# Row means taken off the down weights once, and the last tiles of the last segment summed chunk by chunk

## The chip, the cores and the metric

The kernel runs on one core of one Trainium2 chip. The metric is the device time of one execution in microseconds (us), the median of several runs. The engines are called as in the profile: PE (TensorE), DVE (VectorE), ACT (ScalarE), POOL (GpSimd), SP (SyncE, which issues most DMAs).

## What is computed

The input `u` is 4 sequences of 1024 tokens with 256 features. Two blocks follow, each between two layernorms without gain or bias, with a residual sum:

```python
x = x + layernorm(mamba2(layernorm(x)))
x = x + layernorm(ffn(layernorm(x)))

gate = x @ Wg.T;  up = x @ Wu.T            # Wg, Wu: 2048 x 256, dequantized from 4-bit codes
out  = (gelu_tanh(gate) * up) @ Wd.T       # Wd: 256 x 2048, dequantized from 4-bit codes
layernorm(x) = (x - mean(x)) / sqrt(var(x) + 1e-5)
```

The change concerns the very last layernorm, the one over the 256 outputs of `ffn`.

## The kernel before, in words

**Recorded, then ordered.** The kernel does not call the engines directly. A `Recorder` notes every operation (`add`, line 158), finds out which earlier operations it depends on, gives it a modelled duration (`weigh`, line 227) and, in `issue` (line 260), a list scheduler sets the order of each engine's instructions. So all instructions stand at line 347 in the profile, and are told apart by the names of their tiles. Among the operations that are ready, the one with the lowest `rank` (line 363) goes first: operations of the feed-forward part that are not on PE have rank 5, its PE products 25 + 10 s for segment s, the down products 27 + 10 s, the mixer of segment 2 has 10, the unpacking of the down weights 24. When two operations on different engines touch the same PSUM bank, the recorder orders them, also if both only read (line 185). Buffers come from pools (line 84) and are handed out nearly in the order in which they were asked for; pool "yo" has one buffer, "act" three, "fo" two.

**Segments.** The 4096 tokens are cut into 9 segments (line 25): two of 256 tokens, then seven of 512. For each there is a mixer (the Mamba-2 block, line 646) and a feed-forward part (`ffn`, line 960). A chunk is 128 tokens, so a segment has NC = 2 or 4 chunks.

**Feed-forward part.** The 2048 hidden features are NN = 16 tiles of 128. In segments 0 and 1, `widen(n)` makes one tile: gate and up products on PE, gelu on ACT, the product of both on DVE, and `narrow((n,))` adds the tile's share of the down product. From segment 2 on, `widen_pair(j)` makes tiles j and j + 8 at once by a scheme with seven products, and `narrow((j, j + 8))` follows. `narrow` loops over the chunks and adds, for each, the given tiles to `pd`, a half of a PSUM bank: chunks 0 and 1 share one bank, chunks 2 and 3 the other. A matmul in float32 appears as two PE instructions in the profile. The weights of the down product are `wd`, 128 partitions x 2 x 2048; tile n = 2 tt + par is the slice `wd[:, par, 256 tt : 256 tt + 256]`, a hidden feature per partition and the 256 outputs along it.

**Finish.** `finish(i)` (line 1059) does the last layernorm of a chunk: `bn_stats` and `bn_aggr` on DVE give mean and variance of `pd`, two POOL operations on one column give `q = (var + eps)^-0.5`, DVE computes `(pd - mean) * q` into "fo", POOL adds the residual, SP stores. The way out of the mixer (`way_out`, line 904) does the corresponding layernorm of the first block with a mean square only: its weights `wo` have their row means taken off in `prepare_wo` (line 572). Its steps are Square with an accumulated sum on ACT, two small POOL operations and one DVE operation.

**Unpacking.** `unpack` (line 585) turns the 4-bit codes into float weights. For the down weights it is recorded after the first four steps of segment 0's `ffn` (line 1123). Its codes lie in `big`, its signs in the "yo" buffer, and it writes `wd` in pieces of 512 columns: the first two on DVE, the others on POOL.

Of the kernel before, what the change touches and what calls it, by code (L numbers as in the profile page):

```python
# [12 lines left out]
AF = mybir.ActivationFunctionType  # L13
ALU = mybir.AluOpType
PSUM = bass.MemoryType.PSUM

P = 128
EPS = 1e-5
NB, L, DM = 4, 1024, 256
# [5 lines left out]
SEGS = [(0, 0, 256), (0, 256, 256)] + [(b, 0, 512) for b in range(1, NB)] + \  # L25
# [11 lines left out]
NN = MLP // P  # L37
# [336 lines left out]
def mamba_ffn_kernel(  # L374
# [19 lines left out]
    r = Recorder(tc.nc)  # L394
# [4 lines left out]
    def pool(name, shape, k=1, ahead=2, of=None, dtype=F32):  # L399
        of = of or sb  # L400
        return Pool([of.tile(shape, dtype, name=f"{name}{j}") for j in range(k)], ahead)

    def fixed(name, shape):
        return pool(name, shape).get()
# [30 lines left out]
    def get(tag):  # L435
        return pools[tag].get()
# [37 lines left out]
    for name, shape, src in (("dtb", [P, NH], dt_bias), ("aneg", [P, NH], a_log),  # L474
                             ("cw", [P, NF, 4], conv_w), ("cb", [P, NF], conv_b),
                             ("dsk", [P, DI // P], d_skip), ("nw", [P, DI // P], norm_w)):
        t = small_loads[name] = fixed(name, shape)
# [49 lines left out]
    wd = fixed("wd", [P, 2, MLP])  # L527
# [19 lines left out]
    def stats_of(rows, who="m"):  # L547

        n = len(rows)
        mv = get("mv" + who)[:, :n, :]  # L550
        for i, row in enumerate(rows):
            st = get("st" + who)
            r.vector.bn_stats(st, row)
            r.vector.bn_aggr(mv[:, i, :], st)
        return mv
# [29 lines left out]
    def unpack(pack, scale, room, dst, spare, own, by_product=True):  # L585

        w, sc = room[:, :MLP].bitcast(I32), room[:, MLP:]
        r.sync.dma_start(out=w, in_=pack)
        if by_product:
            few = dst.rearrange("p k n -> p (k n)")[:8, :MLP]
            r.sync.dma_start(out=few, in_=scale)
        else:
            r.sync.dma_start(out=sc, in_=scale.unsqueeze(1).to_broadcast([8, 16, MLP]))
        by, lo, hi = [spare[:, k * 512 : (k + 1) * 512] for k in range(3)]
        sg = get("yo").rearrange("p c t -> p (c t)").bitcast(I32)  # L600
        r.scalar.copy(by.bitcast(U8), w.bitcast(U8).rearrange("p (n k) -> p n k", k=4)[:, :, 0])
        by, lo, hi = by.bitcast(I32), lo.bitcast(I32), hi.bitcast(I32)
        r.vector.tensor_scalar(lo, by, 0x07070707, 2, ALU.bitwise_and, ALU.logical_shift_left)
        r.vector.tensor_scalar(sg, by, 4, 0x80808080 - (1 << 32),
                               ALU.logical_shift_left, ALU.bitwise_and)
        r.vector.tensor_tensor(lo, lo, sg, ALU.bitwise_or)
        r.vector.tensor_scalar(hi, by, 2, 0x1C1C1C1C, ALU.logical_shift_right, ALU.bitwise_and)
        r.vector.tensor_scalar(sg, by, 0x80808080 - (1 << 32), None, ALU.bitwise_and)
        r.vector.tensor_tensor(hi, hi, sg, ALU.bitwise_or)
        for q in range(4):  # L610
            cols = slice(q * 512, (q + 1) * 512)
            by_column = sc[:, cols]
            if by_product:
                bank = banks_d.get()
                r.tensor.matmul(bank, lhsT=spread, rhs=few[:, cols], start=True, stop=True)
                if q < own:
                    by_column = bank
                else:
                    r.scalar.copy(by_column, bank)
            for par, codes in enumerate((lo, hi)):  # L620
                (r.vector if q < own else r.gpsimd).tensor_tensor(
                    dst[:, par, cols], codes.bitcast(F8)[:, cols], by_column, ALU.mult)

    def weight_sums():
# [333 lines left out]
    def ffn(s):  # L960
# [3 lines left out]
        if s < 2:  # L964
            at = big[s].rearrange("p (n t) -> p n t", t=T)
            inter = [[at[:, n, i * P : (i + 1) * P] for i in range(NC)] for n in range(NN)]
        else:


            at = [big[0][:, k * 2 * TMAX : (k + 1) * 2 * TMAX] for k in range(4)]  # L970
# [4 lines left out]
        def widen(n):  # L975
            cols = slice(n * P, (n + 1) * P)
            bank = banks_f.get("full")


            parts = NC if s == 0 else 1  # L980
            step = T // parts
            for i in range(parts):
                for m, w in enumerate((wg, wu)):
                    for kk in range(2):
                        r.tensor.matmul(bank[:, m * T + i * step : m * T + (i + 1) * step],
                                        lhsT=w[:, kk, cols],
                                        rhs=xfT[s][:, kk, i * step : (i + 1) * step],
                                        start=(i == 0 and m == 0 and kk == 0),
                                        stop=(kk == 1), skip_group_check=True)
            a = get("act")  # L990
            r.scalar.activation(a, bank[:, :T], AF.Gelu_apprx_tanh)
            r.vector.tensor_tensor(at[:, n, :], a, bank[:, T : 2 * T], ALU.mult)

        def fetch(k):
            r.sync.dma_start(out=blocks[k % 2], in_=stock[k])
# [40 lines left out]
        def widen_pair(j):  # L1036
            a = big[1][:, j % 4 * 2 * TMAX : (j % 4 + 1) * 2 * TMAX]
            for k, bank in enumerate(seven(0, j)):
                r.scalar.activation(a[:, k * TMAX : (k + 1) * TMAX], bank, AF.Gelu_apprx_tanh)
            for k, bank in enumerate(seven(1, j)):  # L1040
                cols = slice(k * TMAX, (k + 1) * TMAX)
                r.vector.tensor_tensor(at[j % 4][:, cols], a[:, cols], bank, ALU.mult)

        def narrow(tiles):


            r.key = ("down", s)
            if not tiles[0]:
                v_["pd"] = [banks_d.get() for i in range(0, NC, 2)]
            for i in range(NC):  # L1050
                pd = v_["pd"][i // 2][:, i % 2 * DM : (i % 2 + 1) * DM]
                for n in tiles:
                    tt, par = divmod(n, 2)
                    r.tensor.matmul(pd, lhsT=inter[n][i], rhs=wd[:, par, tt * DM : (tt + 1) * DM],
                                    start=(n == 0 and i % 2 == 0), stop=(n == NN - 1),
                                    skip_group_check=True)
            r.key = ("ffn", s)

        def finish(i):
            x = xs[s]  # L1060
            pd = v_["pd"][i // 2][:, i % 2 * DM : (i % 2 + 1) * DM]
            om = stats_of([pd], "f")

            q = get("rsf")[:, 0:1]
            r.gpsimd.tensor_scalar(q, om[:, 0, 1:2], 1.0, EPS * 2.0 ** -12, ALU.mult, ALU.add)
            r.gpsimd.tensor_tensor(q, q, mhalf[:, 0:1], ALU.pow)
            o = get("fo")
            r.vector.tensor_scalar(o, pd, om[:, 0, 0:1], q, ALU.subtract, ALU.mult)
            r.gpsimd.tensor_tensor(o, o, x[:, i, :], ALU.add)
            r.sync.dma_start(out=out[r0 + i * P : r0 + (i + 1) * P, :], in_=o)  # L1070

        if s < 2:
            steps = [lambda n=n: widen(n) for n in range(NN)]
            steps += [lambda n=n: narrow((n,)) for n in range(NN)]
        else:
            steps = [token_sums]
            for j in range(NN // 2):
                if j % 2 == 0:
                    steps.append(lambda k=j // 2: fetch(k))
                steps.append(lambda j=j: widen_pair(j))  # L1080
                steps.append(lambda j=j: narrow((j, j + 8)))
        return steps + [lambda i=i: finish(i) for i in range(NC)]

    r.key = ("small", 0)
# [4 lines left out]
    def do(kind, s, steps):  # L1089
        for step in steps:  # L1090
            r.key = (kind, s)
            step()
# [25 lines left out]
    for s in range(ns):  # L1118
        steps = ffn(s)
        if s == 0:  # L1120
            do("ffn", 0, steps[:4])
            r.key, r.floor = ("w", 1), 24000.0
            unpack(d_pack, d_scale, big[1], wd, big[0][:, 5 * MLP // 4 :], 2, False)
            r.floor = 0.0
            steps = steps[4:]
        do("ffn", s, steps)
        if s == 0:
            r.key, r.floor = ("w", 2), 75000.0
            weight_sums()
            r.floor = 0.0  # L1130
        if s + 2 < ns:
            do("mix", s + 2, mix[s + 2])
# [52 lines left out]
```

## Time and profile before

| | us |
|---|---|
| median of 3 runs | 1045.73 |
| lowest and highest run | 1041.16 and 1045.83 |
| the profiled execution | 1042.28 |
| its span, first to last instruction | 1040.6 |
| granted TensorE clock, mean | 0.99 |
| matmuls of the down product (`d<-wd,big`) | 1024 instructions, 254.9 busy |
| first down product starts | 119.8 |
| ACT table loads | 50, 64.2 busy |

The profile comes from one execution. Its page has a table of busy time, a strip in 40 slices, the DMA queues, the chain of work that ended last, and the groups of instructions. In a group or a timeline line, `out<-in` are the names of the tiles written and read, without their numbers; `x4` says how many instructions were merged, and what stands in brackets is how long the engine had been idle before, and the instruction whose end released it. In a table of stretches each engine has its busy time and number of instructions, and then come the granted TensorE clock (1.00 is full speed), the DMA engines' busy share and GB/s. Tiles that matter: `d` are the PSUM banks of the down product, `a` and `f` the other PSUM banks, `stf`, `mvf`, `rsf` and `fo` belong to `finish`, `one` and `xn` to the mixer's way out, `act` and `big` hold hidden features.

### The profile page before, as it was taken

How to read it: one execution, taken by the hardware profiler on the slowest of the kernel's cores; microseconds unless marked ns; L12 is line 12 of the kernel's file. 1: busy time of each engine (PE TensorE's matmuls, PEld its weight loads, DVE VectorE, ACT ScalarE, POOL GpSimd, SP SyncE). 2: the span in 40 equal slices, each digit the busy share in tenths (PEclk: the TensorE clock that was granted, in tenths of full speed). 3: DMA queues.
4: the chain of work that ended last, by engine and by line, in shares of the span. 5: the costliest groups of instructions: out<-in, count | busy, mean ns of one | idle time of the engine just before them, and what ended most of it. 6: DMA issues, size and time to landing. Idle time of an engine off the chain costs nothing. (4 is left out here: it accounts for less than half of the span.)

```text
span 1040.6 us, 14518 instructions
## 1 busy us (share of the span) xinstructions
PE 1010.6 (97%) x5174; PEld 809.5 (78%) x5174; DVE 652.1 (63%) x1443; ACT 471.3 (45%) x1106; POOL 327.7 (31%) x519
## 2 busy tenths in 40 slices
PE   7989999989999999999999999999999999999996
PEld 6678877866788768876788778877787778888885
DVE  5776695457766775767665857586667765433432
ACT  4536245426663375444654726365435743331330
POOL 1754853440143222503440146102640145002002
PEclk8999999989999999999999999999999999999999
DMA  7014151414032143113312423123221430232400
GB/s 258 3 41 143 74 180 42 172 31 130 23 111 100 44 150 117 37 63 132 111 52 77 145 101 124 72 92 111 83 91 72 132 132 16 76 142 81 151 2 20
DMA packets 39456, 97.16 MB, mean 93 GB/s; under 512 B 3800, under 2 KB 29896, under 8 KB 35272
## 3 DMA queue, kind: packets, MB, share of 16 engines
q1 hardware_dynamic: 38808, 96.22, 27.1%
q8 instruction: 40, 0.66, 0.3%
q14 instruction: 32, 0.26, 0.1%
q10 hardware_dynamic: 576, 0.02, 0.0%
HBM read 84.58 MB, written 11.66 MB: 92 GB/s over the span
## 5 line engine op out<-in xcount | busy, mean ns | idle before, releaser
L347 PE MATMUL f<-wide 128*128 128x256 f32 x880 | 255.4, 384 | 0.6 <-DVE f L347 0.3
L347 PE MATMUL d<-wd,big 128*128 128x256 f32 x1024 | 254.9, 381 | 0.0
L347 PE MATMUL f<-xfT,wide 128*128 128x256 f32 (+1 forms) x1024 | 249.9, 356 | 2.6 <-ACT tail L347 1.3
L347 PEld LDWEIGHTS d<-wd,big 128*128 128x128 f32 x1024 | 189.8, 190 | 31.9 <-issue 9.2
L347 PEld LDWEIGHTS f<-xfT,wide 128*128 128x128 f32 x1024 | 172.0, 191 | 31.2 <-issue 9.2
L347 PEld LDWEIGHTS f<-wide 128*128 128x128 f32 x880 | 161.5, 191 | 35.2 <-issue 12.7
L347 DVE TENSOR_TENSOR f<-f,sums 128x256 f32<-128x256 f32 x216 | 92.5, 429 | 97.9 <-PE f L347 89.9
L347 PE MATMUL a<-xnT,win 128*128 128x512 f32 (+1 forms) x300 | 136.5, 584 | 1.3 <-DVE xw L347 1.0
L347 DVE SCALAR_TENSOR_TENSOR xc<-a,cw,xc 128x511 f32<-128x511 f32 (+1 forms) x135 | 97.9, 727 | 8.9 <-ACT tail L347 6.6
L347 ACT ACTIVATE big<-f 128x512 f32<-128x512 f32 x108 | 63.0, 597 | 79.8 <-DVE f L347 56.0
L347 PEld LDWEIGHTS a<-xnT,win 128*128 128x128 f32 x300 | 55.0, 190 | 44.7 <-issue 37.1
L347 DVE TENSOR_TENSOR big<-big,f 128x512 f32<-128x512 f32 x108 | 72.8, 683 | 26.9 <-PE f L347 16.5
L347 ACT ACTIVATE e<-e,ncs 128x128 f32<-128x128 f32 x240 | 73.9, 390 | 20.8 <-POOL e L347 20.7
L347 ACT COPY f<-f 128x256 f32<-128x256 f32 x104 | 37.5, 361 | 79.8 <-PE f L347 68.7
L347 POOL TENSOR_TENSOR state<-state,dec 128x512 f32<-128x512 f32 x24 | 25.0, 1043 | 149.6 <-PE a L347 128.7
L347 ACT ACT_TABLE_LOAD x50 | 64.2, 1283 | 3.6 <-issue 2.8
L347 POOL TENSOR_SCALAR_AFFINE_SELECT e<-e 128x1024 f32<-128x1024 f32 x30 | 33.1, 1104 | 102.1 <-DMA e<-rows 101.8
L347 POOL TENSOR_SCALAR rsf<-mvf 128x1 f32<-128x1 f32 x32 | 6.9, 215 | 179.3 <-DVE mvf L347 154.2
L347 ACT ACTIVATE xc<-a,cb,cw 128x512 f32<-128x512 f32 (+1 forms) x45 | 34.3, 761 | 50.8 <-PE a L347 50.8
L347 PE MATMUL a<-wo,y 128*128 128x256 f32 x232 | 55.8, 382 | 1.3 <-DVE x L347 1.2
L347 ACT ACTIVATE th<-xc 128x512 f32<-128x512 f32 (+1 forms) x54 | 31.6, 586 | 45.1 <-DVE xc L347 31.1
L347 POOL TENSOR_TENSOR y<-xc,dsk 128x512 f32<-128x512 f32 x32 | 33.6, 1064 | 56.1 <-DVE xc L347 28.1
(242 smaller groups left out, 1402.0 us busy)
## 6 DMA issues: line engine op xcount, KB each, us to landing
wide<-stock SPq DMA_DIRECT2D x28, 1792.0 KB, 7.4
e<-rows SPq DMA_DIRECT2D x30, 512.0 KB, 4.0
r<-rows SPq DMA_DIRECT2D x54, 128.0 KB, 4.0
stock<-sums SPq DMA_DIRECT2D x8, 512.0 KB, 2.8
out_dram<-fo SPq DMA_DIRECT2D x32, 128.0 KB, 1.7
x<-in_u_dram SPq DMA_DIRECT2D x7, 512.0 KB, 3.9
stock<-wide SPq DMA_DIRECT2D x6, 512.0 KB, 6.5
win<-in_w_in_dram SPq DMA_DIRECT2D x2, 512.0 KB, 6.4
```

The source lines that it names most:

```text
L347: getattr(getattr(self.nc, st.queue), st.name)(*[real(a) for a in st.args], **{k: real(a) for k, a in st.kwargs.items()})
```

## The change

There are three edits.

1. A new function `centre_wd`, called once, right after the down weights are unpacked. For each of the 16 tiles of `wd` ACT sums the 256 outputs of every hidden feature, scaled by -1/256, into one column (the element-wise result goes to a "yo" buffer and is not used), and then adds that column to the tile in place. The down product of such weights has a mean of zero over its 256 outputs.
2. `finish` takes the mean square of `pd` on ACT (Square with an accumulated sum; the element-wise result goes to an "act" buffer and is not used), computes `q` on POOL as before, and makes `pd * q + x` in one DVE operation. The mean, `bn_stats`, `bn_aggr` and the POOL addition are gone.
3. In the last segment, the tiles of the pairs 6 and 7 are no longer added by two calls of `narrow`, each over all chunks, but by one call over four tiles: all four for chunk 0, then for chunk 1, and so on.

```diff
+    def centre_wd():
+        n = NN
+        mean = fixed("centre", [P, n])
+        at = lambda tt, par: wd[:, par, tt * DM : (tt + 1) * DM]
+        for k in range(n):
+            junk = get("yo").rearrange("p c t -> p (c t)")[:, :DM]
+            r.scalar.activation(junk, at(*divmod(k, 2)), AF.Identity, scale=-1.0 / DM,
+                                 accum_out=mean[:, k : k + 1])
+            r.scalar.activation(at(*divmod(k, 2)), at(*divmod(k, 2)), AF.Identity,
+                                 bias=mean[:, k : k + 1])
...
         def finish(i):
             x = xs[s]
             pd = v_["pd"][i // 2][:, i % 2 * DM : (i % 2 + 1) * DM]
-            om = stats_of([pd], "f")
-            q = get("rsf")[:, 0:1]
-            r.gpsimd.tensor_scalar(q, om[:, 0, 1:2], 1.0, EPS * 2.0 ** -12, ALU.mult, ALU.add)
+            small = get("rsf")
+            so, q = small[:, 0:1], small[:, 1:2]
+            junk = get("act")
+            r.scalar.activation(junk, pd, AF.Square, scale=1.0 / math.sqrt(DM), accum_out=so)
+            r.gpsimd.tensor_scalar(q, so, 1.0, EPS * 2.0 ** -12, ALU.mult, ALU.add)
             r.gpsimd.tensor_tensor(q, q, mhalf[:, 0:1], ALU.pow)
             o = get("fo")
-            r.vector.tensor_scalar(o, pd, om[:, 0, 0:1], q, ALU.subtract, ALU.mult)
-            r.gpsimd.tensor_tensor(o, o, x[:, i, :], ALU.add)
+            r.vector.scalar_tensor_tensor(o, pd, q, x[:, i, :], ALU.mult, ALU.add)
             r.sync.dma_start(out=out[r0 + i * P : r0 + (i + 1) * P, :], in_=o)
...
-                steps.append(lambda j=j: narrow((j, j + 8)))
+                if s < len(SEGS) - 1 or j < NN // 2 - 2:
+                    steps.append(lambda j=j: narrow((j, j + 8)))
+                elif j == NN // 2 - 1:
+                    steps.append(lambda j=j: narrow((j - 1, j + 7, j, j + 8)))
...
             unpack(d_pack, d_scale, big[1], wd, big[0][:, 5 * MLP // 4 :], 2, False)
+            centre_wd()
```

## The prediction

> **What bounds the kernel now.** First the page's table of busy time, then the busy time by stretches, then the instructions in order of time around the two places that the change touches.
>
> ```profile
> PE 1010.6 (97%) x5174; PEld 809.5 (78%) x5174; DVE 652.1 (63%) x1443; ACT 471.3 (45%) x1106; POOL 327.7 (31%) x519
> ```
>
> PE (TensorE) is the bound. It is idle for 30.0 us in all: 8.6 after its last matmul, and the other 21.4 in a few places (9.7 in the first 90 us, 1.5 at 113, 4.8 between 215 and 230, the rest in crumbs below 0.5). Work taken off DVE or POOL, or put on ACT, moves the time only in those places, or where it makes a new one. The stretches that matter (columns: span, busy us and instructions of PE, weight load, DVE, ACT, POOL; granted clock; DMA):
>
> ```profile
> 112.00:120.00 8.00, 6.47 (x57) 6.43 (x57) 7.32 (x12) 1.75 (x6) 7.75 (x11) 1.00 0.01 2
> 120.00:125.00 5.00, 5.00 (x29) 4.36 (x28) 2.30 (x7) 1.77 (x5) 3.04 (x6) 1.00 0.26 107
> 125.00:130.00 5.00, 5.00 (x26) 3.48 (x25) 0.40 (x3) 0.83 (x2) 2.17 (x4) 1.00 0.45 165
> 130.00:140.00 10.00, 10.00 (x42) 7.69 (x41) 9.65 (x18) 4.43 (x8) 5.82 (x8) 1.00 0.50 180
> 215.00:230.00 15.00, 10.16 (x43) 7.65 (x42) 8.53 (x25) 3.59 (x12) 6.56 (x16) 0.82 0.20 54
> 1032.00:1040.60 8.60, 0.00 (x0) 0.00 (x0) 2.88 (x8) 0.00 (x0) 5.07 (x10) 0.78 0.18 61
> ```
>
> Here the reader sees room on ACT from 112 to 140 (8.8 us busy of 28), where the centring must go; an idle, slowed PE around 220; and a tail in which PE does nothing and POOL is busiest. The tail in order of time (start, duration):
>
> ```profile
> 1014.98 17.00 PE L347 MATMUL d<-wd,big 128*128 128x256 f32 x78
> 1030.29 0.76 DVE L347 BATCH_NORM_STATS2 stf<-d 128x6 f32<-128x256 f32 x2 [11.17 <-PE d L347]
> ...
> 1032.02 0.76 DVE L347 BATCH_NORM_STATS2 stf<-d 128x6 f32<-128x256 f32 x2 [0.75 <-PE d L347]
> ...
> 1034.79 0.46 POOL L347 TENSOR_SCALAR rsf<-mvf 128x1 f32<-128x1 f32 x2
> 1035.33 1.06 POOL L347 TENSOR_TENSOR rsf<-rsf,mhalf 128x1 f32<-128x1 f32 x2
> 1035.91 1.20 DVE L347 TENSOR_SCALAR fo<-d,mvf,rsf 128x256 f32<-128x256 f32 x2 [2.10 <-POOL rsf L347]
> 1036.53 1.40 POOL L347 TENSOR_TENSOR fo<-fo,x 128x256 f32<-128x256 f32 x2
> ```
>
> PE ends at 1031.98 with 78 instructions of the last down product (a matmul is two, so 39 of them at 17.00 / 39 = 0.436 us). The finishes go by pairs: chunks 0 and 1 lie in one bank and start when both are summed, at 1030.29; chunks 2 and 3 at 1032.02. POOL decides the end: the adds of chunks 0 and 1 hold it until 1034.7, so the second pair's first POOL step waits until 1034.79, and the last add ends at 1037.93. The last store and what follows it take 1040.60 - 1037.93 = 2.67 us.
>
> **Part 1: the tail.** A finish loses on DVE bn_stats (420 ns), bn_aggr (169) and the 534 ns TENSOR_SCALAR, and on POOL the 774 ns add; it gains on ACT a Square with its accumulator and on DVE one SCALAR_TENSOR_TENSOR. The same four operations at the same size stand in the mixer's way out, here with nothing in their way:
>
> ```profile
> 221.31 0.38 ACT L347 ACTIVATE xn<-a 128x256 f32<-128x256 f32 x1 [3.85 <-DVE one L347]
> 221.59 0.20 ACT L347 ACTIVATION_READ_ACCUMULATOR xn<-a 128x1 f32 x1
> ...
> 221.86 0.19 POOL L347 TENSOR_TENSOR one<-one,one 128x1 f32<-128x1 f32 x1
> 222.13 0.55 POOL L347 TENSOR_TENSOR one<-one,mhalf 128x1 f32<-128x1 f32 x1
> ...
> 222.71 0.48 DVE L347 SCALAR_TENSOR_TENSOR x<-a,one,x 128x256 f32<-128x256 f32 x1 [0.48 <-POOL one L347]
> ```
>
> So one chain is 223.19 - 221.31 = 1.88 us. The question is whether two chunks of one bank overlap. In the way out DVE reads the bank for q, and ACT's Square reads other columns of it only afterwards, though it needs nothing of q:
>
> ```profile
>   ACT xn L347: 50.3, 24
> ```
>
> That is the list of who waited for tile "one": ACT's Squares stood 50.3 us in 24 waits that ended with DVE's read. I take it that chunk 3's Square waits in the same way for chunk 2's DVE output. The second pair: 1032.02 + 1.88 = 1033.90, 0.05 to hand over, + 1.88 = 1035.83, + 2.67 = 1038.50. That is **-2.1 us** against 1040.60. The first pair is done 16 instructions earlier when the last 16 matmuls go chunk by chunk (8 of a bank, 3.5 us, where it was 1.73 us), so its chains run from about 1028.5 to 1032.4. By the old order they would run from 1030.29, mixed with the second pair's on three engines that are each under 1 us busy per chunk; the reorder by itself I price at 0 to 0.3 us. PE loses nothing by it: the last inputs are written by 1019.13, 13 us before the end. The stores take two "fo" buffers; the third output comes about 3 us after the first, whose store landed in 1.7 us, so no wait is added there.
>
> The Trainium skill, page "PSUM — Partial Sum Buffer", section "PSUM bank collisions raise a hardware error", says that two engines may not touch one bank and quadrant at once, reads against reads included, and that guards go by bank. That speaks against the change, which puts two reading engines where one had both reads: with the rule the sum is the -2.1 us above, without it the -3.2 of rival 1. The 50.3 us agree with it.
>
> **Part 2: centring, once.** 16 tiles of 128x256, two ACT operations each. The nearest rows: the Square with accumulator is 0.47 us to the end of the read (221.31 to 221.79); the scaled activation of "wo" at this size is 514 ns with a pointer operand. About 1.0 us a tile with the hand-over, 16 us in all. The tiles share one "yo" buffer, handed out in order, so sums go tile 0 to 15. Tile 0 is unpacked by 113.1, tiles 0 to 3 by about 114, tile 4 by 115.6; the last DVE write into wd, which I take to be tiles 5 and 7, ends at 120.0. On ACT, with the gelus between, tiles 0 to 4 are done by about 119, 5 to 7 by 123.5, then the mixer's copies (123.56 to 124.9) and tiles 8 to 15 by about 134.5. What PE wants, and when:
>
> ```profile
> 119.78 1.03 PE L347 MATMUL d<-wd,big 128*128 128x256 f32 x4
> ...
> 130.64 4.48 PE L347 MATMUL d<-wd,big 128*128 128x256 f32 x20
> ```
>
> Segment 0 has two chunks, so a tile is four PE instructions. Tile 0 is wanted at 119.78, 22 instructions have gone by 125.4 (into tile 5), tile 10 is wanted near 134.5, tile 11 at 136.67. Every tile is there one to five us early, so nothing is lost; but a gelu or copy may stand up to 0.5 us behind a centring operation, and ACT may wait in order for the write that ends at 120.0. I take **+0.3**; the ends are 0 and the whole cover of 119.8 to 125.4, 22 x 0.217 = 4.8 us. Nothing else in the box of 112 to 140 moves: wd is not read before, and the next user of "yo" comes after 170. Square and Identity ran between gelus with no table load in front (xn at 103.83, xc at 129.12), so none is counted.
>
> **Part 3: the other 28 finishes.** DVE loses 0.65 us and POOL 0.77 us of each, ACT gains 0.58. They lie beside a PE that is 99% busy, and a bank held 2 us longer is wanted again only a widened pair later. Only segment 1's finish falls into an idle stretch, 216.9 to 221.7: its two POOL adds and DVE steps stand ahead of the mixer's rsm, xf and one. Taking 1.46 us from POOL and 1.3 from DVE there I put at **-0.5**; the ends are +0.5 (a Square ahead of the mixer's) and the gap itself, 4.8.
>
> **Sum** -2.1 + 0.3 - 0.5 = -2.3 us: the profiled execution's 1042.28 would become 1040.0. It lies 3.45 under the median of the runs, which spread from 1041.16 to 1045.83; a new median has the same spread, so I put the sum on the median: 1045.73 - 2.3 = **1043.4**. Less than 0.5% (5.2 us) is about what a measurement of this kernel can't tell from no change.
>
> **Rivals.** The issue order is planned from modelled costs, so all of it may shift; these are the ways that have a price.
>
> 1. Bank reads don't serialize. Chunk 3's Square follows chunk 2's by 0.5 us, only POOL's 0.82 us per chunk lies between, and its chain ends near 1034.7: -3.2 in the tail, 1042.3 in all; were chunks freed singly, not by bank, -4.0 and 1041.5. Against it: the 50.3 us, and pairs that started together at 1030.29 and 1032.02. Chance 0.12.
> 2. The stretch at 220 closes. PE is idle 4.8 us there and its clock is 0.82, which costs 10.16 x 0.18 = 1.8 us more. If a new order fills it, -6.6, with the tail and the front -8.4: 1037.3. For it: three engines wait for each other by turns there. Against: the chain is way out, statistics, xf, transposes, which all stay. Chance 0.16.
> 3. ACT is late at 120, and the time is slower. If tile 0 is centred only at 125, PE loses its filler of 4.8 us. The tiles behind it follow at 1.8 us (1.0 us each in the 56% that ACT has free from 130 to 140), so tile 10, wanted at 134.5, comes at 143, and half of the 42 instructions from 130.6 to 144.5 has no cover, 4.6 us. The gap at 220 shows what follows an idle PE: a clock of 0.82 there, 2.4 us with the ten us behind it. 11.8 - 2.6 = +9.2: 1054.9. It decides from the point where tile 0 comes 3 us after 119.78; before that the tail pays for it. For it: ACT's order is fixed beforehand, and one DVE write into wd took 1.51 us where another took 0.81. Against: ACT is busy 1.75 of the 8 us before, and segment 1's products could fill from 125 on. Chance 0.14.
>
> The forecast, a change between -4 and +1, has 0.58. Noise of the median can carry a part of it over the bound, so faster 0.21 (rival 2 and a twentieth), same 0.65, slower 0.14. The range takes in rival 2 and the forecast's spread, and stops short of rival 3's end: 1037.3 to 1049.0.
>
> **What would show it.** Tail: a gap of about 6.5 us after the last matmul; ACT's second Square of a pair released by DVE "fo" and not by PE; POOL under 0.8 us per chunk. Front: ACT busy some 16 us more between 112 and 136, no PE wait on ACT "wd". Middle: DVE 21 and POOL 25 us less, ACT 35 more, PE's sum of busy time unchanged. It is wrong if PE's idle time before the tail leaves 21.4 by more than 3 us.

## The result, and the profile after

The median is 1039.76 us (20 runs, 1035.7 to 1042.6) against 1041.76 of the kernel before on the same chip (20 runs, 1039.88 to 1045.85). The medians lie 2.0 us apart; the ratio on record, which is not that of the two medians, is 0.9977 with a 95% interval of [0.9967, 0.9988]: 2.4 us less, with an interval from 1.2 to 3.4. The profiled execution took 1041.29 us with a span of 1039.2. Its table of busy time:

```profile
PE 1012.9 (97%) x5174; PEld 811.5 (78%) x5174; DVE 634.2 (61%) x1379; ACT 506.0 (49%) x1224; POOL 302.5 (29%) x487
```

PE has the same 5174 instructions; DVE is busy 17.9 us less, POOL 25.2 less, ACT 34.7 more. Of ACT's, 7.7 us are six more table loads (56 instead of 50, 1.28 each); they come with the new finish, as e6 below has 56 without any centring, and e2, the centring alone, has 50. The tail after, in order of time:

```profile
1015.68 17.00 PE L347 MATMUL d<-wd,big 128*128 128x256 f32 x78
...
1029.33 0.38 ACT L347 ACTIVATE act<-d 128x256 f32<-128x256 f32 x1 [18.02 <-PE d L347]
...
1031.26 0.38 ACT L347 ACTIVATE act<-d 128x256 f32<-128x256 f32 x1 [1.46 <-DVE fo L347]
...
1032.78 0.38 ACT L347 ACTIVATE act<-d 128x256 f32<-128x256 f32 x1 [1.04 <-PE d L347]
...
1034.71 0.38 ACT L347 ACTIVATE act<-d 128x256 f32<-128x256 f32 x1 [1.46 <-DVE fo L347]
...
1035.28 0.19 POOL L347 TENSOR_SCALAR rsf<-rsf 128x1 f32<-128x1 f32 x1 [1.11 <-ACT act L347]
1035.55 0.55 POOL L347 TENSOR_TENSOR rsf<-rsf,mhalf 128x1 f32<-128x1 f32 x1
1036.13 0.48 DVE L347 SCALAR_TENSOR_TENSOR fo<-d,rsf,x 128x256 f32<-128x256 f32 x1 [1.45 <-POOL rsf L347]
```

The four Squares (`act<-d`) show who let each one go: the first of a bank is released by PE, the second by DVE's output of the first. One engine works at a time, down to the last DVE output at 1036.13 + 0.48 = 1036.61; the gap after the last matmul is 1039.2 - 1032.68 = 6.5 us, where it was 8.6. The stretches that answer to those of before:

```profile
112.00:120.00 8.00, 6.47 (x50) 6.08 (x50) 7.79 (x14) 3.06 (x11) 7.75 (x8) 1.00 0.16 67
120.00:125.00 5.00, 5.00 (x42) 4.82 (x41) 3.71 (x8) 4.89 (x17) 5.00 (x8) 1.00 0.01 3
125.00:130.00 5.00, 5.00 (x31) 4.00 (x30) 1.46 (x5) 4.90 (x17) 3.08 (x7) 1.00 0.26 105
130.00:140.00 10.00, 10.00 (x41) 7.01 (x41) 5.99 (x10) 8.47 (x25) 4.17 (x6) 1.00 0.73 262
1032.70:1039.20 6.50, 0.00 (x0) 0.00 (x0) 1.43 (x3) 0.95 (x4) 1.48 (x4) 0.87 0.18 61
```

PE is full from 120 to 140, as forecast, while ACT is nearly full from 120 to 130. Nothing here looks like a loss.

**Two measures that leave the start-up out.** The work that before's profile has at 113 us comes 3.8 us later in after's, ahead of any changed operation; in its first 66 us the granted clock is 0.87, in before's 0.92.

```profile
0.00:66.00 66.00, 58.52 (x335) 45.60 (x336) 41.44 (x105) 31.95 (x83) 36.64 (x61) 0.92 0.38 119
```
```profile
0.00:66.00 66.00, 60.57 (x326) 46.70 (x326) 39.70 (x96) 31.43 (x79) 34.00 (x55) 0.87 0.39 119
```

The first line is before, the second after. Ahead of the changed operations all twelve kernels have the same instructions in the same order on PE, ACT, DVE and POOL, and yet this clock lies between 0.87 and 0.95 in their profiles; so spans can't be compared to a microsecond. Below, "the stretch" goes from the matmul behind PE's 1.5 us wait for tile "sz" (113.55 before, 117.35 after) to the first of the last 78 down products; "the tail" from the end of these to the span's end. The stretch is 901.4 before and 898.3 after, the tail 8.6 and 6.5. Before's 901.4 has a second blemish: from 200 to 250 its granted clock is 0.93, in most others 0.97. Kernel e3 below issues the same instructions in this stretch at 0.97 and takes 900.1; that is the base used from here.

### The profile page after: what moved, and what is told of

It is laid out like the page before. It is cut to its first block, busy times and chain, and to the rows that moved or that the text cites. A ratio compares the mean times of both kernels' runs of the same rounds, so it can differ in the third digit from the quotient of the medians.

```text
span 1039.2 us, 14552 instructions
## 1 busy us (share of the span) xinstructions
PE 1012.9 (97%) x5174; PEld 811.5 (78%) x5174; DVE 634.2 (61%) x1379; ACT 506.0 (49%) x1224; POOL 302.5 (29%) x487
## 4 chain that ended last, share of the span: by engine, by line
PE 91%; POOL 4%; DVE 3%; ACT 1%; issue 0%; DMA 0%; POOLq 0%; ACTq 0%; DVEq 0%
PE f L347 39%; PE a L347 30%; PE d L347 22%; DVE xc L347 1%; POOL wide L347 1%; POOL sz L347 1%; POOL rsm L347 1%; DMA aneg<-in_a_log_dram 0%; POOL y L347 0%; POOL sums L347 0%; POOL one L347 0%; DVE f L347 0%; POOL state L347 0%; POOL rsf L347 0%; DVE stm L347 0%
## 5 line engine op out<-in xcount | busy, mean ns | idle before, releaser
L347 DVE TENSOR_TENSOR big<-big,f 128x512 f32<-128x512 f32 x108 | 72.7, 684 | 31.4 <-PE f L347 20.6
L347 POOL TENSOR_SCALAR rsf<-rsf 128x1 f32<-128x1 f32 x32 | 6.1, 191 | 187.6 <-ACT act L347 186.4
L347 POOL TENSOR_TENSOR sz<-sz 128x256 f32<-128x256 f32 x64 | 39.1, 611 | 54.6 <-ACT sz L347 52.9
```

The costliest lines, as they stand in the source:

```text
L347: getattr(getattr(self.nc, st.queue), st.name)(*[real(a) for a in st.args], **{k: real(a) for k, a in st.kwargs.items()})
```

## The experiments

**Theory.** The tail is the chain of one-at-a-time finishes that the prediction worked out. The centring costs more than its +0.3, since it stands on ACT ahead of something that the segment 2 mixer needs, and the lighter finishes give back more than 0.5. **Rivals:** the centring is free and the reorder or the finish has its price; in the tail, banks don't serialize.

| kernel | edits | stretch | tail | ratio to before [95%] |
|---|---|---|---|---|
| before | none | 901.4 (clock 0.93 at 200 to 250) | 8.6 | 1 |
| after | 1, 2, 3 | 898.3 | 6.5 | 0.9977 [0.9967, 0.9988] |
| e1 | 1, 2 | 898.4 | 7.0 | 0.9969 [0.9952, 0.9985] |
| e2 | 1 | 903.9 | 8.6 | 1.0052 [1.0031, 1.0072] |
| e3 | 3 | 900.1 | 6.7 | 0.9983 [0.9967, 0.9999] |
| e4 | 1, 2, 3, last finishes by pairs | 898.5 | 5.5 | 0.9943 [0.9922, 0.9964] |
| e5 | 1 twice, 2, 3 | 921.3 | 6.5 | 1.0192 [1.0165, 1.0219] |
| e6 | 2, 3 | 895.9 | 6.5 | 0.9932 [0.9914, 0.9950] |
| e7 | 1 with a scheduler rule | 900.6 | 8.6 | 1.0000 [0.9986, 1.0015] |
| e8 | e4 with that rule | 895.8 | 5.8 | 0.9916 [0.9900, 0.9931] |
| e9 | 3, no centring, half of 2 | 896.1 | 5.7 | 0.9938 [0.9921, 0.9955] |
| e10 | 3, no centring, other half of 2 | 898.0 (clock 0.93 at 200 to 250) | 8.0 | 0.9955 [0.9940, 0.9969] |

**e1, the third edit undone.**

```diff
-                if s < len(SEGS) - 1 or j < NN // 2 - 2:
-                    steps.append(lambda j=j: narrow((j, j + 8)))
-                elif j == NN // 2 - 1:
-                    steps.append(lambda j=j: narrow((j - 1, j + 7, j, j + 8)))
+                steps.append(lambda j=j: narrow((j, j + 8)))
```

> The change without its third edit: centring and the new finish, but the last eight tiles' share is added by two calls over all chunks, as before. Theory (the two chunks of a bank go one after the other, 1.88 us each, and the two banks' chains run beside each other on engines that are nearly free): the gap from the last matmul to the end is 6.5 to 7.0 us, so the order by chunk is worth at most 0.5 us in this kernel. Rival (the order by chunk carries the gain of the tail): the gap goes back by the 1.7 us by which bank 0 ends later, to about 8.2 us.

**e2, the first edit alone**: `centre_wd` and its call are added to before, the old finish stays.

> The first edit alone: the weights are centred, the finish still computes mean and variance on DVE. Theory (ACT has room from 112 to 140 us): no wait of PE on ACT between 112 and 145 us, ACT 16 to 17 us busier there, the tail as before at 8.6 us, the time within 2 us of before. Rival (centring takes PE's filler): a PE gap of 2 to 5 us that ends on the centred weights, and the time 2 to 8 us above before.

**e3, the third edit alone**: the reorder of the last tiles, with the old finish and no centring.

> The third edit alone: the old finish, no centring, the last 16 matmuls chunk by chunk. Theory (the old tail is a queue on POOL, which two adds of the first bank hold for 4.5 us after that bank is summed; the first bank is now ready 1.7 us earlier): POOL is free just as the second bank's variances come, and the tail goes from 8.6 to about 6.8 us, so this edit alone brings nearly what all three bring. Rival (the edit does nothing by itself): the tail stays within 0.3 us of 8.6.

With the new finish, the reorder takes 0.5 us off the tail (7.0 in e1, 6.5 in after). In e1 the first pair starts late, and then the last output waits for a store buffer:

```profile
1034.72 0.38 ACT L347 ACTIVATE act<-d 128x256 f32<-128x256 f32 x1 [1.10 <-DVE fo L347]
...
1036.56 0.48 DVE L347 SCALAR_TENSOR_TENSOR fo<-d,rsf,x 128x256 f32<-128x256 f32 x1 [0.96 <-DMA out_dram<-fo]
```

With the old finish the reorder takes 1.9 (8.6 before, 6.7 in e3). There the first pair is summed earlier, and its two POOL additions (1.41 us) begin at 1031.24, ahead of PE's end at 1031.98:

```profile
1031.24 1.41 POOL L347 TENSOR_TENSOR fo<-fo,x 128x256 f32<-128x256 f32 x2
...
1032.95 0.46 POOL L347 TENSOR_SCALAR rsf<-mvf 128x1 f32<-128x1 f32 x2 [0.30 <-DVE mvf L347]
...
1034.69 1.40 POOL L347 TENSOR_TENSOR fo<-fo,x 128x256 f32<-128x256 f32 x2
```

POOL is free when the second pair's variance comes (its first step waits 0.30 us for DVE's "mvf"), where before it was POOL that the pair waited for. So edits 2 and 3 are substitutes: either takes away the same POOL queue, and both together bring hardly more than one.

Both readings of e2's expectation missed: the time is 6.1 us above before, and PE has no wait on a centred tile. Its stretch is 3.8 us longer than e3's: the centring has a price that stands nowhere in 112 to 140. Most of it shows 80 us later, from 200 to 250, first e3, then e2:

```profile
200.00:250.00 50.00, 44.85 (x224) 33.76 (x223) 33.05 (x90) 15.51 (x39) 16.99 (x33) 0.97 0.11 34
```
```profile
200.00:250.00 50.00, 41.92 (x209) 31.06 (x208) 29.94 (x82) 15.14 (x40) 19.39 (x34) 0.97 0.11 38
```

PE is idle 5.2 us in the one and 8.1 in the other, at the same clock: 2.9 of the 3.8. The cause is to be found in between, on ACT, in order of time. Before:

```profile
132.39 0.63 ACT L347 ACTIVATE th<-xc 128x512 f32<-128x512 f32 x1 [0.72 <-DVE xc L347]
133.04 1.28 ACT L347 ACT_TABLE_LOAD   x1
134.33 0.23 ACT L347 ACTIVATE dte<-dte 128x32 f32<-128x32 f32 x1
...
144.93 0.25 ACT L347 ACTIVATE dec<-a 128x96 f32<-128x96 f32 x1 [1.34 <-PE a L347]
```

After:

```profile
136.95 0.51 ACT L347 ACTIVATE wd<-wd,centre 128x256 f32<-128x256 f32 x1
...
140.30 1.28 ACT L347 ACT_TABLE_LOAD   x1
141.59 0.23 ACT L347 ACTIVATE dte<-dte 128x32 f32<-128x32 f32 x1
...
153.07 0.25 ACT L347 ACTIVATE dec<-a 128x96 f32<-128x96 f32 x1 [1.40 <-PE a L347]
```

The exponentials of segment 2's step sizes (`dte`) need another table than the gelus around them. In after, all 16 centring tiles (117.1 to 137.5) go ahead of that switch. Taken from the "sz" matmul, `dte` comes at 24.2 us instead of 20.8, and the decays (`dec`), which the mixer waits for, at 35.7 instead of 31.4. The recorder's scheduler does this: `issue` adds 1400 ns to an ACT operation that needs a switch, and drops it from the choice if any other can start within 300 ns. Identity fits every table, so 16 ready tiles keep the switch away, whatever the rank. PE stays full until 150 with other work (segment 1's products and the down products), and the chain that comes late meets it at 220, where it had little else to do already. This last link is only read from the traces; that the place of the centring is the cause is tested next.

**e7, the first edit with a rule in the scheduler**: while an operation that needs a switch is open, the centring is left out of the choice. Its rank is as before.

```diff
+                    if any(st.table not in (None, table) for st in when):
+                        when = {st: t for st, t in when.items() if st.key[0] != "centre"}
                     now = min(when.values())
...
+            r.key = ("centre", 0)
+            centre_wd()
```

> Centring alone, as in the run with only that edit, but the scheduler leaves centring operations out while an operation that needs another ACT table is ready. Theory (the late Exp is what centring costs): the Exp of the step sizes stands ahead of the last five tiles, the decays come at most 33 us after the wait on sz, where they came at 36.1 with centring alone and at 31.4 before, and the stretch falls from 903.9 to between 899 and 902. Rival (it is ACT's load, or the new order as such): the stretch stays at 903 to 905.

```profile
134.98 1.28 ACT L349 ACT_TABLE_LOAD   x1
136.27 0.23 ACT L349 ACTIVATE dte<-dte 128x32 f32<-128x32 f32 x1
136.41 0.49 ACT L349 ACTIVATE wd<-wd,centre 128x256 f32<-128x256 f32 x1
...
148.12 0.25 ACT L349 ACTIVATE dec<-a 128x96 f32<-128x96 f32 x1 [0.24 <-PE a L349]
```

The last five tiles now stand behind the switch. That takes back nearly all of the price: `dec` is 31.4 us behind the "sz" matmul again (148.12 - 116.70), the stretch is 900.6 against 903.9 in e2 and 900.1 without centring, and from 200 to 250 PE is as busy as in e3:

```profile
200.00:250.00 50.00, 44.85 (x230) 34.21 (x229) 33.23 (x88) 15.29 (x40) 17.66 (x33) 0.97 0.11 41
```

The same 32 operations cost 0.5 us instead of 3.8, and the rule that puts five tiles behind the switch is the only difference between the two programs: that the place is the price is shown.

**e5, the centring twice** (a second pass, by its own column, right behind the first).

```diff
...
+            centre_wd("centre")
+            centre_wd("again")
```

> The changed kernel with the centring done twice; the second time takes off means that are zero. Common measure here and below, the stretch: from the matmul with the 1.52 us wait on POOL sz near 115 us to the first of the last 78 down products. It was 901.4 us before, 898.3 in the changed kernel, 903.9 with centring alone. Theory (all centring stands ahead of the step sizes' Exp on ACT, because that needs a table switch and the scheduler puts a switch behind whatever runs without one; the whole of segment 2's mixer is late by that): the Exp and the decays come 10 to 16 us later still, the gap near 220 grows and the stretch gets 6 to 14 us longer than the changed kernel's, about 904 to 912. Rival (ACT simply has room): at most 2 us longer.

The direction is right and the size is not. `dec` comes at 71.9 us behind the "sz" matmul, 36 later than in after, and the stretch is 23.0 us longer than after's. Two stretches of e5 hold most of that:

```profile
118.00:150.00 32.00, 30.05 (x125) 21.90 (x124) 17.41 (x33) 27.02 (x87) 17.20 (x26) 0.84 0.35 132
200.00:250.00 50.00, 37.78 (x191) 27.34 (x189) 23.96 (x51) 13.16 (x40) 23.13 (x37) 0.83 0.13 43
```

PE's busy time times the share of the clock that is missing gives an estimate of what the clock takes: 30.05 x 0.16 + 37.78 x 0.17 = 11.2 us here, 1.3 in after (43.62 x 0.03, at 200 to 250). And PE is idle 2.0 + 12.2 us against 6.4: some 18 of the 23. The expectation had left the clock out. PE doesn't wait for a centred tile even here: its longest wait from 118 to 150, 1.5 us, is for DVE's "xn".

**e6, the change without the first edit.** It leaves the subtraction of the mean out.

```diff
-            centre_wd()
```

> The changed kernel without the centring: new finish and order by chunk, the weights keep their row means. It leaves a part of the computation out, the mean of the last layernorm. Theory (centring costs some 3.8 us in the stretch, and the new finish gains some 5.5 there by itself): the stretch is 893.5 to 896 us, the time 3 to 4 us under the changed kernel. Rival (the new finish gains there only what centring has spoilt): the stretch is 898 to 901 us, and the time that of the changed kernel within 1 us.

The stretch is 895.9: 2.4 us below after (what the centring costs beside the new finish) and 4.2 below e3, which differs only by the finish. So the new finish gives 4.2 before the tail, where 0.5 was forecast. Where it comes from is seen at the finishes of segments 2 to 5. First e3, then e6:

```profile
350.00:375.00 25.00, 22.97 (x94) 16.00 (x93) 22.77 (x55) 12.63 (x30) 8.04 (x15) 1.00 0.36 106
480.00:500.00 20.00, 19.31 (x80) 13.33 (x79) 16.31 (x32) 13.09 (x33) 12.08 (x21) 1.00 0.29 86
```
```profile
350.00:375.00 25.00, 24.00 (x100) 16.71 (x99) 20.49 (x50) 15.52 (x39) 7.10 (x13) 1.00 0.36 106
480.00:500.00 20.00, 19.82 (x86) 14.29 (x85) 14.71 (x25) 14.42 (x40) 8.63 (x14) 1.00 0.17 54
```

PE gains 1.0 us in the first stretch and 0.5 in the second. From 600 to 650 and from 750 to 800 it gains 0.3 and 0.8 more (49.74 to 50.00, and 49.17 to 49.97), and 0.8 at 200 to 250 (44.85 to 45.68). They add up to 3.4 of the 4.2; the other 0.8 was not placed. These are the crumbs of idle time that the prediction had seen and not placed. It took all of them for shorter than 0.5 us; three of before's are not:

```profile
360.43 0.38 PE L347 MATMUL a<-upper,da 128*32 128x128 f32 x2 [0.69 <-ACT sums L347]
...
371.02 0.70 PE L347 MATMUL f<-xfT,wide 128*128 128x256 f32 x2 [0.83 <-ACT big L347]
...
753.27 1.09 PE L347 MATMUL a<-e,xdt 128*64 128x128 f32 x16 [0.72 <-DVE e L347]
```

The second of these waits is still there in e6 (0.94 us); the other two are gone. From 250 us to the last matmul PE is idle 4.6 us in e3 and 2.0 in e6. The expectation had 3.8 us for the centring and 5.5 for the finish; both are smaller, 2.4 and 4.2.

**e9 and e10, half of the lighter finish each**, both with the reorder, without centring, and without the subtraction of the mean. e9 keeps the statistics on DVE and drops POOL's addition; e10 keeps POOL's addition and takes the sum of squares on ACT.

```diff
 # e9
+            om = stats_of([pd], "f")
+            r.gpsimd.tensor_scalar(q, om[:, 0, 1:2], 1.0, EPS * 2.0 ** -12, ALU.mult, ALU.add)
...
             r.vector.scalar_tensor_tensor(o, pd, q, x[:, i, :], ALU.mult, ALU.add)
 # e10
             r.scalar.activation(junk, pd, AF.Square, scale=1.0 / math.sqrt(DM), accum_out=so)
...
+            r.vector.tensor_scalar(o, pd, q, None, ALU.mult)
+            r.gpsimd.tensor_tensor(o, o, x[:, i, :], ALU.add)
...
```

> Halfway between the old and the new finish, without centring, order by chunk: variance on DVE by bn_stats and bn_aggr as before, but one fused DVE output and no POOL addition. It leaves the mean of the last layernorm out. The stretch was 900.1 us with the old finish and 895.9 with the new one, both without centring. Theory (POOL is what the mixer's short steps queue for near each finish, since every finish holds it for two adds in a row per bank): the stretch is 895.5 to 897.5 us. Rival (DVE is, with 0.59 us of statistics per chunk): 898.5 to 900.5 us.

> The other half: mean square on ACT as in the change, but the output in two steps as before, a DVE multiplication and a POOL addition; without centring, order by chunk. It leaves the mean of the last layernorm out. Theory (POOL's adds cost the stretch): 898.5 to 900.5 us. Rival (DVE's statistics do): 895.5 to 897.5 us. Between the two, both engines count.

The stretch is 896.1 in e9 and 898.0 in e10; e10's clock from 200 to 250 is 0.93 where e6 has 0.97, worth 45.4 x 0.04 = 1.8 us, so some 896.2 at an equal clock (an estimate). Either half gives nearly all that both give, so neither reading, that POOL's addition is what delayed PE or that DVE's statistics are, can be the whole of it. PE's idle time from 250 us on is 2.5 us in e9 and 2.2 in e10. In e3, where it is 4.6, every such wait of more than 0.1 us ends on DVE or ACT and none on POOL; since these two may have waited for POOL before, which engine held up the finishes of segments 2 to 5 stays open. In the tail of e9 statistics and output are both on DVE and it takes 5.7 us, less than after's.

**e4, the last finishes by pairs.** In the last segment both Squares of a bank come first, then the POOL steps of both chunks, then both DVE outputs.

```diff
+        def finish_two(k):
+            for i in (2 * k, 2 * k + 1):
...
+                r.scalar.activation(junk, pd, AF.Square, scale=1.0 / math.sqrt(DM), accum_out=so)
+            for i, pd, so, q in two:
+                r.gpsimd.tensor_scalar(q, so, 1.0, EPS * 2.0 ** -12, ALU.mult, ALU.add)
+                r.gpsimd.tensor_tensor(q, q, mhalf[:, 0:1], ALU.pow)
+            for i, pd, so, q in two:
...
+                r.vector.scalar_tensor_tensor(o, pd, q, x[:, i, :], ALU.mult, ALU.add)
...
```

> The changed kernel with one more edit: in the last segment the two chunks of a bank are finished together, both Squares first, then POOL, then both DVE outputs. Every engine has the same instructions in the same order as in the changed kernel; only who waits for whom differs. Theory (the second chunk's Square waits for the first chunk's DVE output only because both read one bank): the second Square starts 0.5 us after the first, the tail falls from 6.5 to about 5.4 us. Rival (the wait has another cause, the buffer of the discarded squares or the output buffers): the tail stays at 6.5 us.

```profile
1031.80 0.38 ACT L347 ACTIVATE act<-d 128x256 f32<-128x256 f32 x1 [2.61 <-PE d L347]
...
1032.18 0.38 ACT L347 ACTIVATE act<-d 128x256 f32<-128x256 f32 x1
...
1033.22 0.48 DVE L347 SCALAR_TENSOR_TENSOR fo<-d,rsf,x 128x256 f32<-128x256 f32 x1 [2.06 <-POOL rsf L347]
...
1034.13 0.48 DVE L347 SCALAR_TENSOR_TENSOR fo<-d,rsf,x 128x256 f32<-128x256 f32 x1 [0.42 <-POOL rsf L347]
```

The order of instructions on each engine is that of after; only the recorder's order between ACT's and DVE's reads of a bank is another. The second Square now comes 0.38 us behind the first and not 1.9, and the tail is 5.5 instead of 6.5 us. So what stands between two chunks of a pair in after is the order of the two engines' reads, and nothing that an engine is busy with. The runs put e4 further below after (0.9943 against 0.9977, 3.5 us) than this 1.0 us; the stretch is the same in both profiles, so what the rest would be is not shown.

**e8, the best of both**: e4 with e7's rule.

> The kernel with the last two chunks of a bank finished together, with the same rule in the scheduler. Theory: stretch from 898.5 to about 895, tail 5.5 us as in that run, so the time falls by another 3 us, to 0.991 of before. Rival: the stretch stays at 898.5 within 1 us and the ratio at 0.994.

```profile
131.91 1.28 ACT L349 ACT_TABLE_LOAD   x1
133.21 0.23 ACT L349 ACTIVATE dte<-dte 128x32 f32<-128x32 f32 x1
133.34 0.49 ACT L349 ACTIVATE wd<-wd,centre 128x256 f32<-128x256 f32 x1
...
138.34 0.51 ACT L349 ACTIVATE wd<-wd,centre 128x256 f32<-128x256 f32 x1
...
145.05 0.25 ACT L349 ACTIVATE dec<-a 128x96 f32<-128x96 f32 x1
```

The switch comes first and the last tiles are centred behind it. The stretch is 895.8, as without centring (895.9), the tail 5.8, and the median 1034.67 against 1042.77, a ratio of 0.9916 [0.9900, 0.9931]: 8.1 us below before, and the lowest ratio of these kernels (its interval overlaps those of e6 and e9, which leave a part of the computation out).

## Why the prediction was right, and where it was not

The time was forecast at -2.3 us and came out at -2.4 [-3.4, -1.2]; against the median shown (1045.73) the forecast's 1043.4 stands 3.6 us above the measured 1039.76, because the median of before was itself 1041.76 in 20 runs. Putting the sum on the median of three runs was the step that missed here; the 1040.0 that the prediction had worked out from the profiled execution lies 0.2 from the measured median. The change is below 0.5%, as forecast, but 20 runs do tell it from no change, which the prediction doubted. That the sum came out is luck in part: two of its terms were wrong by about as much, with opposite signs.

- **Part 1, -2.1, right**: 8.6 to 6.5, with the mechanism as told. Of its steps, the second Square released by DVE "fo" (1031.26 and 1034.71) and the POOL steps at 0.19 + 0.55 = 0.74 us a chunk are in the trace. Rival 1 falls: e4 shows the price of taking turns at a bank, 1.0 us in the tail. The section "PSUM bank collisions raise a hardware error" of the Trainium skill's page "PSUM — Partial Sum Buffer" rules out that two engines touch one bank and quadrant at once, two reads included; the 1.0 us is what the kernel pays for keeping to that by turns. What the chip would do otherwise no run here shows: none lets two engines read a bank at once.
- **The reorder, 0 to 0.3**: 0.5 beside the new finish, a little over the end. That it alone would bring 1.9 (8.6 to 6.7 in e3), and that the new finish alone brings 1.6 (8.6 to 7.0 in e1), was not seen: what is worth nothing as the second edit may be worth everything as the first.
- **Part 2, +0.3, the step that failed in its mechanism**: "Nothing else in the box of 112 to 140 moves." PE's wants were all met (no PE wait there, so rival 3's place was wrong), but the exponentials behind the table switch moved, by 3.4 us, and with them segment 2's mixer. The centring itself went about as forecast: it kept ACT busy for 14.9 us, where 16 were forecast, and its last tile was done 20.1 us behind the "sz" matmul (137.46 - 117.35), where 21.0 were forecast (134.5 - 113.55). The prediction looked at who waits for the centring's output, not at what waits behind it on its engine. It did say that no table load comes in front of Square and Identity, and this is true; it is just why they were let through ahead of the one that needed a load. The term measures +3.8 (e3 to e2), +2.4 beside the new finish (e6 to after), +0.5 behind the switch (e3 to e7).
- **Part 3, -0.5, the term that was mis-sized**: -4.2 (e3 to e6), -5.6 (e2 to after). "They lie beside a PE that is 99% busy": of the 4.6 us that PE was idle behind 250 us, 2.6 went with the old finish, and 0.8 more at 220.
- **Rival 2** did not come: PE is idle 6.4 us from 200 to 250 in after, with 5.2 in e3.
- **The warning sign** (PE's idle time before the tail leaving 21.4 by more than 3 us) did not show: it is 19.8. It is blind to two errors that cancel. Another sign met its number by chance: ACT is 34.7 us busier, as forecast (35), but 7.7 of these are the six table loads, of which the prediction counted none; the operations themselves came out lighter (27.0).

Summed at an equal clock, the profiles give 898.3 - 900.1 = -1.8 in the stretch and -2.1 in the tail, -3.9 in all, somewhat outside what the runs give (-2.4 [-3.4, -1.2]). A run takes 1.7 us longer than its span before and 1.9 after, which explains 0.2 of it. In the same way e2 is 6.1 us slower than before in the runs, but only 3.8 slower than e3 in the stretch. Each stretch comes from one execution, and the start-up makes several microseconds of difference between executions; that this is the whole of it was not tried.

## What to carry to other kernels

For an added operation, look not only at when its result is wanted but at what stands behind it on its engine; an operation that fits any ACT table can hold back one that needs a switch, and the bill comes where PE has nothing else to do, here 80 us later. A PE at 99% still has its idle time in places: before pricing relief of other engines at nothing, find the crumbs and see which operations lie beside them. And when two engines read one PSUM bank, let each take its reads in a row instead of by turns; it cost two loops and gave 1.0 us at the end of the kernel.

## What the runs showed of the hardware

- A table switch costs what its load takes. ACT_TABLE_LOAD is 1.28 us and the next ACTIVATE starts 1.29 us after its start (133.04 to 134.33; 140.30 to 141.59); behind 44 of before's 50 loads the next instruction starts within 0.02 us of the load's end. The Trainium skill's page "ScalarE: Activation LUTs", section "What ACT_TABLE_LOAD costs", gives about 1.38 us of DRAIN beside it, 2.66 in all; no such time is in these rows, and the measurement decides.
- The granted clock can fall with no long PE wait ahead of it. From 210 to 235 in after PE is busy 18.94 of 25 us and no wait of it is longer than 1.7 us, and the clock from 230 to 240 is 0.83. It is a patch of 3.4 us at half the clock, with 1.00 on both sides; in the 3.4 us ahead of it PE is busy for 1.23. The 0.93 of before and of e10 from 200 to 250 is a patch of 6.8 us at 0.50 in each (from 224.5 and from 228.2). The lines are after's:

```profile
230.00:240.00 10.00, 8.96 (x40) 6.98 (x41) 4.30 (x14) 2.96 (x8) 0.00 (x0) 0.83 0.01 2
232.00:235.40 3.40, 3.40 (x10) 2.78 (x11) 1.49 (x5) 2.08 (x6) 0.00 (x0) 0.50 0.00 0
```

- The clock of the first 66 us differs between executions of the same instructions: 0.87 in after, e1 and e10, 0.90 in e2, e4 and e7, 0.92 before, 0.94 in e8, 0.95 in e3, e5, e6 and e9. By the estimate above it takes 58.52 x 0.08 = 4.7 us before and 60.57 x 0.13 = 7.9 in after: 3.2 of the 3.8 us between them at the "sz" matmul. It is not all that differs at the start: e9, with 0.95, reaches that matmul last of all, at 118.47.
